# Laying out the setup of a two-layer transformer kernel by VectorE's time, and cutting its norms into pieces

## The chip, the cores and the metric

The kernel runs on one core of a Trainium2 chip. The metric is the device time of one execution in microseconds; of several runs the median is taken. Everything is computed in 32-bit floats.

## The reference

Two transformer layers follow one another on x of shape (8, 512, 256), with a condition of shape (8, 256) and a context of shape (8, 64, 192). The kernel's text calls them block 0 and block 1. Cut to what matters:

```
# layer 0 (16 heads of 16)
mod = silu(cond) @ adaln_w.T + adaln_b          # split in nine: shift, scale, gate of sa, ca, ff
h = ln(x) * (1 + scale_sa) + shift_sa
q, k, v = ln(heads(h)), ln(heads(h)), heads(h)  # no projection, a norm of every head
x = x + gate_sa * unheads(softmax(q k^T / 4) v)
h = ln(x) * (1 + scale_ca) + shift_ca
kv = ctx @ cond_w.T + cond_b
x = x + gate_ca * (softmax((h wq^T)(kv wk^T)^T / 4)(kv wv^T) @ ca_out_w.T + ca_out_b)
h = ln(x) * (1 + scale_ff) + shift_ff
x = x + gate_ff * ((silu(h @ w1.T) * (h @ w3.T)) @ w2.T)
# layer 1 (16 heads of 64, rotary positions on q and k)
a = ln(x) * (1 + cond @ g1 + ..) + (cond @ b1 + ..)
x = x + attention(a, a) ;  x = x + attention(adaln1(x), ln(ctx)) ;  x = x + gelu(adaln2(x) w1) w2
```

## The kernel before

Each of the 8 batch elements ("batches") of x is kept in SBUF as four tiles of 128 tokens by 256 features. Block 0 is worked as a list of slots, which `run_blocks` walks through. In slot i it issues the early functions of the slot's block, the scores of block i (TensorE), the values of block i−1, and then whatever `beside` holds for slot i, a dictionary to which `at(i, fn)` appends. Within this loop the order on TensorE, VectorE, ScalarE and GpSimd is exactly the order in which the code issues instructions (`manual_schedule`); SyncE's queue, which issues the DMAs, is ordered by a scheduler. An instruction that waits therefore holds up everything behind it on its own engine.

A cycle has 18 slots. Batch b's self-attention in block 0 takes 16 slots from `base = 18 b` on: four head groups, each with four blocks of 128 keys. The other two slots of a cycle hold the two cross-attention blocks of the batch before. So in the steady state three batches are in work at once:

- `batch1(b)`: self-attention. `norm` normalizes and modulates x into `h`; `head_centre`, `head_var` and `head_scale` do the norm of every head (a power on GpSimd, 16 or 32 elements per partition); `queries_keys` transposes (L500) and evicts q on ScalarE (L503) and k on VectorE (L504). Exponentials are L520; `group_back` divides by the sums (L547 to L549).
- `batch2(b)`: cross-attention, from `base = 18 (b+1)`. `prepare` at base+3 normalizes x to z (statistics L183/L184, rstd L174 on VectorE, its power L175 on GpSimd, four applications L187) and adds a row to x (L395). `turn` at base+5 transposes z (L362) and evicts it with scale and shift (L363). `queries` at base+6 and base+7 are two projections with w_q (L609 evicts them). `inverse` takes the reciprocal of the sums and sends it through DRAM and back over all partitions (DMAs `rec`, `rb`); `scaled` multiplies (L652), and the output projection (w_o, in bank `ps_D`) opens the next cycle but one.
- `batch3(b)`: the feed-forward part, from `base = 18 (b+2)`, a few slots later for some batches and two earlier for the last: `prepare` at base+5, `turn` at base+7, eight `up` steps, then four `down` steps, whose results are added with a gate (L418, L420).

Ahead of slot 0 and within the first 18 slots lies the setup. `linear_rows` multiplies the conditions' 8 rows with 512 columns of the modulation's weights and adds the biases on VectorE (L258). The first modulation row is spread over the 128 partitions by a matmul with ones. `to_columns` transposes rows into columns (L263). `awake` issues matmuls whose results nobody reads. `modulation` (slot 1) makes the other rows, `context0` (3), `keys0` (5) and `values0` (7 to 10) the cross-attention's keys and values, `modulation1` (12) and `context1` (14) the conditions and the context of block 1. This setup up to slot 0 is ordered by the scheduler.

In the second cycle `keys1(p)`, at slots 20, 22, .. 34, makes the cross-attention keys of block 1: two matmuls, rotary positions on VectorE and GpSimd (L735 to L739), and a store to DRAM (`k_d`, L759). At slot 36 `open_ff` loads the feed-forward weights.

All matmuls go through one helper, so they share L109 in the profile. Accumulators are the banks `ps_S`, `ps_O`, `ps_D` and `ps_X`.

Of the kernel before, what the change touches and what calls it, by code (L numbers as in the profile page):

```python
# [10 lines left out]
F32 = mybir.dt.float32  # L11
# [67 lines left out]
def fast_path(ctx: ExitStack, tc: tile.TileContext, a: dict, out: bass.AP):  # L79
# [109 lines left out]


# [20 lines left out]
    nc.sync.dma_start(cT, a["cT"].rearrange("(k p) b -> p k b", p=P))  # L211
    mod = sp.tile([B, 9 * D], F32, name="mod")
    nc.sync.dma_start(mod, a["adaln_b"].to_broadcast([B, 9 * D]))
    adaw = sp.tile([P, 2, 9 * D], F32, name="adaw")

# [3 lines left out]
    load_k(adaw[:, :, 0 : 2 * D], a["adaln_wT"][:, 0 : 2 * D])  # L219
    load_x(0)  # L220
    nc.sync.dma_start(cols, a["cols"])
    load_k(adaw[:, :, 2 * D : 3 * D], a["adaln_wT"][:, 2 * D : 3 * D])
    load_k(adaw[:, :, 3 * D :], a["adaln_wT"][:, 3 * D :])

    ctxT = sp.tile([96, 2, B * T], F32, name="ctxT")
    condw = sp.tile([96, 2, D], F32, name="condw")
    wk0 = sp.tile([P, 2, D], F32, name="wk0")
    wv0 = sp.tile([P, 2, D], F32, name="wv0")
    gb = sp.tile([B, 4 * D], F32, name="gb")
    gbw = sp.tile([P, 2, 4 * D], F32, name="gbw")  # L230
    ctx_in = sp.tile([P, 4, CD], F32, name="ctx_in")

    def load_rest():
        load_k(ctxT, a["ctxT"], 96)
        load_k(condw, a["cond_wT"], 96)
        nc.sync.dma_start(ctx_in, a["ctx"].rearrange("(t p) d -> p t d", p=P))
        load_k(wk0, a["wkT"])
        load_k(wv0, a["wvT"])
        nc.sync.dma_start(rows, a["rows"].to_broadcast([P, 5 * D]))
        nc.sync.dma_start(gb, a["gb_b"].to_broadcast([B, 4 * D]))  # L240
        load_k(gbw, a["gb_w"])
        load_k(w_q0, a["wqT"])
        load_k(w_o0, a["woT"])
        for b in range(1, B):
            load_x(b)


    scT = sp.tile([P, 2, B], F32, name="scT")
    nc.scalar.activation(scT, cT, AF.Tanh, scale=0.5)
    nc.vector.scalar_tensor_tensor(scT, scT, 1.0, cT, ALU.add, ALU.mult)  # L250
    nc.vector.tensor_scalar_mul(scT, scT, 0.5)

    def linear_rows(dst, xT, w, lo, n):

        ps = bank_x()
        for kc in range(2):
            mm(ps[:B, :n], xT[:, kc, :], w[:, kc, lo : lo + n], kc == 0, kc == 1)
        nc.vector.tensor_tensor(dst[:, lo : lo + n], ps[:B, :n], dst[:, lo : lo + n], ALU.add)  # L258

    def to_columns(dst, src, chunks):  # L260
        ps = bank_x()
        for i, lo in enumerate(chunks):
            nc.tensor.transpose(ps[:, i * B : (i + 1) * B], src[:, lo : lo + P], ident[:B, :B])  # L263
        nc.vector.tensor_copy(dst.rearrange("p c b -> p (c b)"), ps[:, : len(chunks) * B])

    def awake(n):

        ps = bank_s()
        for _ in range(n):
            mm(ps[:, 0, 0:256], ident, chk.rearrange("p i c -> p (i c)"))  # L270

    awake(4)
    linear_rows(mod, scT, adaw, 0, 512)
    nc.vector.tensor_scalar_add(mod[:, SC_SA : SC_SA + D], mod[:, SC_SA : SC_SA + D], 1.0)
    first_mod = bank_x()
    mm(first_mod, ones, mod[0:1, 0 : 2 * D])
    linear_rows(mod, scT, adaw, 512, 256)
    nc.sync.dma_start(modd[:, 0 : 3 * D], mod[:, 0 : 3 * D])
    awake(13)
    for h in hs:  # L280
        nc.gpsimd.memset(h, 0.0)
        nc.gpsimd.memset(h[:, :, :, HD0 : HD0 + 1], 1.0)
    nc.vector.tensor_copy(qk_cols, cols[:, 0:2])

    def modulation():
        for lo in range(3 * D, 9 * D, 512):
            linear_rows(mod, scT, adaw, lo, 512)

        nc.vector.tensor_scalar_mul(mod[:, G_FF : G_FF + D], mod[:, G_FF : G_FF + D], 0.5)
        nc.sync.dma_start(modd[:, 3 * D :], mod[:, 3 * D :])  # L290
        to_columns(modT, mod, [lo + k * P for lo in (SH_CA, SC_CA, SH_FF, SC_FF) for k in range(2)])
        for lo in (2, 6):
            nc.vector.tensor_scalar_add(modT[:, lo : lo + 2, :], modT[:, lo : lo + 2, :], 1.0)
# [4 lines left out]
    def context0():  # L298
        nc.gpsimd.memset(vb0, 0.0)
        for m in range(2):  # L300
            ps = bank_x()
            for kc in range(2):
                mm(ps, condw[:, kc, m * P : (m + 1) * P], ctxT[:, kc, :], kc == 0, kc == 1)
            nc.vector.tensor_scalar_add(kvT[:, m, :], ps, col("condb")[:, m : m + 1])

    def keys0():
        for m in range(2):
            ps = bank_x()
            for kc in range(2):
                mm(ps, wk0[:, kc, m * P : (m + 1) * P], kvT[:, kc, :], kc == 0, kc == 1)  # L310
            for e in range(2):
                nc.vector.tensor_scalar(kb0[:, m, :, e, :], ps.rearrange("p (b t) -> p b t", b=B),
                                        col("bk")[:, m : m + 1], col("parity")[:, e : e + 1], ALU.add, ALU.mult)
# [12 lines left out]

    def modulation1():

        for lo in range(0, 4 * D, 512):
            linear_rows(gb, cT, gbw, lo, 512)  # L330
        gbT = sp.tile([P, 8, B], F32, name="gbT")
        to_columns(gbT, gb, [k * P for k in range(8)])
# [11 lines left out]
    def context1():  # L344
        for k in range(2):
            ps = bank_x()
            for t in range(4):
                nc.tensor.transpose(ps[:96, t * P : (t + 1) * P], ctx_z[:, t, k * 96 : (k + 1) * 96], ident)
            nc.vector.tensor_scalar(ctxzT[:, k, :], ps[:96, :], col("lncw")[:96, k : k + 1],
                                    col("lncb")[:96, k : k + 1], ALU.mult, ALU.add)  # L350
# [15 lines left out]
    def normed_in_pieces(pool, b, eps):  # L366

        z = pool.tile([P, NT, D], F32, tag="z", name="z", bufs=1)
        st = small.tile([P, NT, 6], F32, tag="st", name="st")
        mv = small.tile([P, NT, 2], F32, tag="mv", name="mv")  # L370
        x, r = xs[b], {}

        def stats(t0):
            for t in range(t0, t0 + 2):
                nc.vector.bn_stats(st[:, t, :], x[:, t, :])
            for t in range(t0, t0 + 2):
                nc.vector.bn_aggr(mv[:, t, :], st[:, t, :])
            if t0:
                r[0] = rstd_of(mv[:, :, 1], NT, eps)

        def apply():
            for t in range(NT):
                nc.vector.tensor_scalar(z[:, t, :], x[:, t, :], mv[:, t, 0:1], r[0][:, t : t + 1],
                                        ALU.subtract, ALU.mult)

        return z, [lambda: stats(0), lambda: stats(2), apply]
# [53 lines left out]
    def batch1(b):  # L440
# [3 lines left out]
        def norm(half=None):  # L444

            if not half:
                s["bc"] = bc = wk.tile([P, 3 * D], F32, tag="bc", name="bc")
                spread(bc, b, SH_SA, 3 * D)
                s["h"] = hs[b % 2]
                s["hv"] = s["h"][:, :, :, 0:HD0]  # L450
                s["ln"] = ln = wk.tile([P, NT, D], F32, tag="ln", name="ln", bufs=1)
                layernorm(ln, xs[b], EPS0)
            lo, n = (0, D) if half is None else (half * P, P)
            eng, rows_ = (nc.gpsimd, s["bc"]) if b else (nc.vector, first_mod)
            ln = s["ln"][:, :, lo : lo + n]
            eng.tensor_tensor(ln, ln, rows_[:, None, D + lo : D + lo + n].to_broadcast([P, NT, n]), ALU.mult)
            lv = ln.rearrange("p t (h d) -> p t h d", d=HD0)
            shift = rows_[:, lo : lo + n].rearrange("p (h d) -> p h d", d=HD0)
            eng.tensor_tensor(s["hv"][:, :, lo // HD0 : (lo + n) // HD0], lv,
                              shift[:, None].to_broadcast([P, NT, n // HD0, HD0]), ALU.add)  # L460

        def head_centre(c):

            if c == 0:
                s["z"] = wk.tile([P, NT, DX], F32, tag="zx", name="zx", bufs=1)
                nc.gpsimd.memset(s["z"][:, :, D:DX], 0.0)
            hv = s["hv"][:, :, 8 * c : 8 * c + 8]
            z = s["z"][:, :, c * P : (c + 1) * P]
            zv = z.rearrange("p t (h d) -> p t h d", d=HD0)
            sh = [P, NT, 8]  # L470
            mean = small.tile(sh, F32, tag="mean", name="mean", bufs=2)
            nc.vector.tensor_reduce(mean, hv, AX.X, ALU.add)
            nc.vector.tensor_scalar_mul(mean, mean, 1.0 / HD0)
            nc.vector.tensor_tensor(zv, hv, mean[:, :, :, None].to_broadcast([*sh, HD0]), ALU.subtract)
# [1661 lines left out]
```

## Time and profile before

| | |
|---|---|
| median of 3 runs | 2459.03 us (2456.31 to 2459.05) |
| profiled execution, own time | 2458.86 us |
| its span | 2457.1 us |
| TensorE busy | 2409.4 us (98%) |
| VectorE / ScalarE / GpSimd busy | 1070.0 / 875.8 / 859.1 us |
| mean granted clock of TensorE | 0.995 |
| DMA | 84.33 MB, 34 GB/s on average |
| first scores of slot 0 / 18 / 36 start at | 25.52 / 101.06 / 170.88 us |

The span runs from the first to the last recorded instruction. Busy times count the records of an engine; a record of TensorE that runs at half the clock counts as busy for twice as long. The profile shows block 0 in about the first third of the span; the rest is block 1.

### The profile page before, as it was taken

How to read it: one execution, taken by the hardware profiler on the slowest of the kernel's cores; microseconds unless marked ns; L12 is line 12 of the kernel's file. 1: busy time of each engine (PE TensorE's matmuls, PEld its weight loads, DVE VectorE, ACT ScalarE, POOL GpSimd, SP SyncE). 2: the span in 40 equal slices, each digit the busy share in tenths (PEclk: the TensorE clock that was granted, in tenths of full speed). 3: DMA queues.
4: the chain of work that ended last, by engine and by line, in shares of the span. 5: the costliest groups of instructions: out<-in, count | busy, mean ns of one | idle time of the engine just before them, and what ended most of it. 6: DMA issues, size and time to landing. Idle time of an engine off the chain costs nothing.

```text
span 2457.1 us, 28357 instructions
## 1 busy us (share of the span) xinstructions
PE 2409.4 (98%) x10938; PEld 1151.5 (47%) x10938; DVE 1070.0 (44%) x2074; ACT 875.8 (36%) x1115; POOL 859.1 (35%) x537
## 2 busy tenths in 40 slices
PE   8999999999999999999999999999999999999999
PEld 3323444434435543444444443434345555566665
DVE  4555444444434534343434343434335666651210
ACT  2555545555462124333333333333332221222221
POOL 3542332332201026343434344444433443531110
PEclk9999999999999999999999999999999999999999
DMA  5121000000001100000000000000113222210000
GB/s 184 32 76 34 17 11 12 21 7 16 13 6 39 56 1 23 19 18 19 19 19 19 19 19 19 19 19 19 36 56 101 68 67 62 68 53 29 22 18 23
DMA packets 84448, 84.33 MB, mean 34 GB/s; under 512 B 42416, under 2 KB 58736, under 8 KB 84296
## 3 DMA queue, kind: packets, MB, share of 16 engines
q1 hardware_dynamic: 83688, 81.88, 10.7%
q8 instruction: 88, 1.44, 0.2%
q10 hardware_dynamic: 616, 0.55, 0.1%
q14 instruction: 56, 0.46, 0.1%
HBM read 72.36 MB, written 10.04 MB: 34 GB/s over the span
## 4 chain that ended last, share of the span: by engine, by line
PE 91%; DVE 2%; DMA 2%; ACT 2%; issue 1%; POOL 1%; SPq 1%; POOLq 0%; DVEq 0%; ACTq 0%
PE ps_X L109 37%; PE ps_S L109 23%; PE ps_D L109 14%; PE ps_O L109 14%; DMA rb<-rec 1%; PE ps_X L362 1%; ACT p L520 1%; POOL p L1148 1%; SPq L1141 1%; DMA rec<-rec 1%; DVE t L738 1%; PE ps_X L500 0%; ACT hT L363 0%; PE ps_X L542 0%; POOL rstd L491 0%
## 5 line engine op out<-in xcount | busy, mean ns | idle before, releaser
L109 PE MATMUL ps_S<-q,k 32*128 32x512 f32 (+1 forms) x3072 | 432.2, 627 | 7.0 <-ACT p L520 3.4
L908 ACT ACTIVATE p<-ps_S 128x1024 f32<-128x1024 f32 x256 | 248.2, 1022 | 522.2 <-PE ps_S L109 520.3
L520 ACT ACTIVATE p<-ps_S 128x1024 f32<-128x1024 f32 x256 | 248.2, 1021 | 259.9 <-PE ps_S L109 259.0
L109 PEld LDWEIGHTS ps_S<-q,k 32*128 32x128 f32 (+1 forms) x3072 | 160.2, 185 | 244.6 <-issue 134.4
L887 DVE TENSOR_TENSOR t<-ps_X,rope_c 128x512 f32<-128x512 f32 x126 | 87.2, 692 | 349.9 <-PE ps_X L109 349.9
L927 DVE TENSOR_TENSOR sm<-sm,p 128x1024 f32<-128x1024 f32 x128 | 191.8, 1541 | 58.5 <-ACT p L908 58.5
L890 POOL TENSOR_TENSOR q<-t 128x512 f32<-128x512 f32 x32 | 40.7, 1273 | 406.2 <-DVE t L888 406.2
L175 POOL TENSOR_TENSOR rstd<-rstd,mhalf 128x4 f32<-128x4 f32 x49 | 49.8, 1016 | 364.8 <-DVE rstd L174 363.4
L923 POOL TENSOR_TENSOR sm<-p 128x1024 f32<-128x1024 f32 x64 | 149.5, 2362 | 37.8 <-ACT p L908 37.8
L109 PE MATMUL ps_X<-hT,w 128*128 128x512 f32 x344 | 160.3, 601 | 0.9 <-ACT hT L363 0.4
L739 POOL TENSOR_TENSOR q<-t,t 128x512 f32<-128x512 f32 x72 | 94.9, 1319 | 174.3 <-DVE t L738 163.1
L109 PE MATMUL ps_O<-p,h 128*32 128x512 f32 x1024 | 139.0, 615 | 0.5 <-ACT oT L533 0.5
L109 PE MATMUL ps_O<-p,v 128*64 128x512 f32 x512 | 138.0, 617 | 0.0
L109 PE MATMUL ps_D<-p,v 128*64 128x512 f32 x512 | 131.6, 592 | 0.0
L411 DVE TENSOR_TENSOR x<-ps_X,x 128x512 f32<-128x512 f32 x27 | 18.7, 691 | 241.3 <-PE ps_X L109 241.3
L109 PE MATMUL ps_X<-hT,w_sa_wq 128*128 128x512 f32 x256 | 115.9, 595 | 3.0 <-ACT hT L363 3.0
L109 PE MATMUL ps_X<-w_sa_wv,hT 128*128 128x512 f32 x256 | 118.0, 604 | 0.0
L109 PE MATMUL ps_X<-w_sa_wo,oT 128*128 128x256 f32 x512 | 114.5, 382 | 0.1
L109 PE MATMUL ps_X<-hT,w_sa_wk 128*128 128x512 f32 x248 | 112.4, 596 | 0.0
L109 PE MATMUL ps_S<-hT,w_ff_w 128*128 128x512 f32 x256 | 111.3, 593 | 0.0
L491 POOL TENSOR_TENSOR rstd<-var,mhalf 128x32 f32<-128x32 f32 (+1 forms) x17 | 87.3, 5134 | 68.6 <-ACT t L692 41.7
L109 PEld LDWEIGHTS ps_X<-w_sa_wo,oT 128*128 128x128 f32 x512 | 96.0, 190 | 24.2 <-issue 11.4
(256 smaller groups left out, 3536.5 us busy)
## 6 DMA issues: line engine op xcount, KB each, us to landing
rb<-rec SPq DMA_DIRECT2D x128, 128.0 KB
rb<-rec_d SPq DMA_DIRECT2D x124, 128.0 KB
x<-in_x_dram SPq DMA_DIRECT2D x8, 512.0 KB
rb<-rec SPq DMA_DIRECT2D x16, 256.0 KB
out_dram<-x SPq DMA_DIRECT2D x15, 256.0 KB
bc<-modd SPq DMA_DIRECT2D x8, 384.0 KB
gate<-modd SPq DMA_DIRECT2D x16, 128.0 KB
k_d<-q SPq DMA_DIRECT2D x8, 256.0 KB
```

What stands on the lines that cost most here:

```text
L109: nc.tensor.matmul(o, lhsT, rhs, start=start, stop=stop)
L175: nc.gpsimd.tensor_tensor(r[:, :n], r[:, :n], mhalf[:, :n], ALU.pow)
L362: nc.tensor.transpose(ps[:, t * P : (t + 1) * P], z[:, t, k * P : (k + 1) * P], ident)
L491: nc.gpsimd.tensor_tensor(r, s["var", c][:, :, hd], half, ALU.pow)
L520: nc.scalar.activation(pr[u], pss[u], AF.Exp, scale=HD0 ** -0.5)
L738: nc.vector.tensor_tensor(t2[d], ps[src], sn[src].to_broadcast([64, *shape[1:]]), ALU.mult)
L739: nc.gpsimd.tensor_tensor(dst, t1, t2, ALU.add)
L887: nc.vector.tensor_tensor(c, ps, rope_c, ALU.mult)
L890: nc.gpsimd.tensor_tensor(r[0], ec, os, ALU.subtract)
L908: nc.scalar.activation(pr, pss[u], AF.Exp, scale=HD1 ** -0.5)
L923: nc.gpsimd.tensor_tensor(sm, s["p", g, 0, u], s["p", g, 1, u], ALU.add)
L927: nc.vector.tensor_tensor(s["sm", g, u], s["sm", g, u], s["p", g, t, u], ALU.add)
```

## The change

The change edits the issue order and the cutting of block 0's work; block 1's own phases issue what they issued.

- **Setup in program order.** The manual order now begins ahead of the setup. The first modulation weights come in two DMAs from ScalarE's queue, batch 0's x in four. The modulation is held as a tile of four groups of 32 rows: eight products of 32 columns with 32 zero-padded conditions, in place of six with 8 rows. Batch 0's modulation row is made on TensorE alone, from its condition repeated over 128 columns, plus ones times bias, plus ones. `awake` runs with 6, 16, 3 and 3 matmuls, in bank O. Fills with zeros are cut to the parts that need them.
- **First heads of batch 0.** The first 8 heads are cut by parity: the even ones go ahead of slot 0 (256 elements per partition, their scaling on VectorE), the odd ones lie in slots 0 and 1, the other 8 heads in slots 2 to 4.
- **The other setup steps** lie in other slots: `modulation` 1, its columns 3, its end 4, `context0` 4 and 5, `keys0` 7 and 9 (half of its eviction on ScalarE), `values0` 10, 11, 14, 15, the context's norm 10, 11, 13, `modulation1` 15, its columns 16, `context1` 16 and 17, the rest of `modulation1` at slot 54.
- **Norms of block 0 in three pieces** (statistics of two tiles; of the other two, and rstd; application): for `batch1` at three successive slots, for `batch2` at base+3, +4, +5, with `turn` at base+6 and the queries at base+7 and +8; for `batch3` at base+4, +5, +7 (the last batch: all at base+5).
- **`keys1(p)`** at slots 22 to 29, one a slot, their stores four slots later, with five buffers.

```diff
+    def norm_pieces(dst, x, eps, width=D):
+        s = {}
+        def stats(t0):
...
+            for t in range(t0, t0 + 2):
+                nc.vector.bn_stats(s["st"][:, t, :], x[:, t, :])
+            for t in range(t0, t0 + 2):
+                nc.vector.bn_aggr(s["mv"][:, t, :], s["st"][:, t, :])
+            if t0:
+                s["r"] = rstd_of(s["mv"][:, :, 1], NT, eps)
+        def apply():
+            d = dst()
...
+        return [lambda: stats(0), lambda: stats(2), apply]
...
+    ms.enter_context(tc.manual_schedule(engines={ENG.PE, ENG.DVE, ENG.Activation, ENG.Pool}))
+    nc.sync.dma_start(cT, a["cT"].rearrange("(k p) b -> p k b", p=P))
+    for k in range(2):
+        nc.scalar.dma_start(adaw[:, k, 0 : 2 * D], a["adaln_wT"][k * P : (k + 1) * P, 0 : 2 * D])
+    for t in range(NT):
+        nc.sync.dma_start(xs[0][:, t, :], a["x"][0][t * P : (t + 1) * P, :])
...
+    awake(6)
+    for k in range(2):
+        mm(first_mod, sc0[:, k, :], adaw[:, k, 0 : 2 * D], k == 0, False)
+    mm(first_mod, ones, mod[0:1, 0 : 2 * D], False, False)
+    mm(first_mod[:, D : 2 * D], ones, chk[0:1].rearrange("p i c -> p (i c)"), False, True)
+    awake(16)
-    awake(4)
-    linear_rows(mod, scT, adaw, 0, 512)
-    nc.vector.tensor_scalar_add(mod[:, SC_SA : SC_SA + D], mod[:, SC_SA : SC_SA + D], 1.0)
-    first_mod = bank_x()
-    mm(first_mod, ones, mod[0:1, 0 : 2 * D])
-    linear_rows(mod, scT, adaw, 512, 256)
-    nc.sync.dma_start(modd[:, 0 : 3 * D], mod[:, 0 : 3 * D])
-    awake(13)
...
     def modulation():
-        for lo in range(3 * D, 9 * D, 512):
-            linear_rows(mod, scT, adaw, lo, 512)
+        ps = bank_x()
+        for k in range(2):
+            for j in range(4):
+                mm(ps[32 * j : 32 * j + 32, :], sc32[:, k, :], adaw[:, k, 2 * D * j : 2 * D * j + 2 * D], k == 0, k == 1)
+        nc.vector.tensor_tensor(mod[:, 0 : 2 * D], ps, mod[:, 0 : 2 * D], ALU.add)
...
-                        at(-1, lambda: head_scale(0, 0))
-                        at(0, lambda: head_scale(0, 1))
-                        at(0, lambda: norm(1))
+                            first_modulated(0, 0)
+                            head_centre(0, 0)
+                            head_var(0, 0)
+                            head_scale(0, 0, nc.vector)
...
+                        at(0, lambda: first_modulated(0, 1))
+                        at(0, lambda: head_centre(0, 1))
+                        at(1, lambda: head_var(0, 1))
+                        at(1, lambda: head_scale(0, 1))
...
-                        at(i - 10, norm)
+                        for m in range(3):
+                            at(i - 11 + m, lambda m=m: norm(m))
...
-        at(base + 3, prepare)
-        at(base + 5, turn)
-        at(base + 6, lambda: queries(0))
-        at(base + 7, lambda: queries(1))
+        for n in range(3):
+            at(base + 3 + n, lambda n=n: prepare(n))
+        at(base + 6, turn)
+        at(base + 7, lambda: queries(0))
+        at(base + 8, lambda: queries(1))
...
-        at(base + 5, prepare)
-        at(base + 7, turn)
+        for n, i in enumerate((5, 5, 5) if b == B - 1 else (4, 5, 7)):
+            at(base + i, lambda n=n: prepare(n))
+        later.append((base + 7, turn))
...
-        at(CYCLE + 2 + 2 * p, lambda p=p: keys1(p))
+        at(CYCLE + 4 + p, lambda p=p: keys1(p))
+        at(CYCLE + 8 + p, lambda p=p: store_keys1(p))
```

## The prediction

> **What bounds the kernel now.** I read the page's busy times first:
>
> ```profile
> PE 2409.4 (98%) x10938; PEld 1151.5 (47%) x10938; DVE 1070.0 (44%) x2074; ACT 875.8 (36%) x1115; POOL 859.1 (35%) x537
> ```
>
> The span is 2457.1 us, so TensorE is idle for 47.7 us in all. The table of windows says where these are, and where busy time is slow time (PEclk is the column after POOL):
>
> ```profile
> 20.00:30.00 10.00, 4.11 (x19) 1.81 (x20) 3.65 (x6) 2.71 (x3) 6.49 (x4) 0.72 1.04 358
> 30.00:40.00 10.00, 9.81 (x32) 2.00 (x28) 2.85 (x5) 2.46 (x3) 5.61 (x2) 0.76 0.79 252
> 80.00:100.00 20.00, 17.74 (x92) 6.48 (x94) 11.43 (x34) 8.93 (x13) 9.49 (x4) 0.83 0.24 64
> 150.00:200.00 50.00, 45.76 (x256) 16.52 (x258) 26.73 (x67) 28.60 (x35) 26.39 (x13) 0.93 0.31 107
> 200.00:250.00 50.00, 49.88 (x238) 17.93 (x231) 24.20 (x62) 28.03 (x37) 13.65 (x8) 1.00 0.03 7
> ```
>
> From 200 us on TensorE has 49.88 of 50 us: nothing to win there, but any wait put there goes straight to the end. Before 200 us there are idle gaps, and three spells at half clock: smaller windows show 0.50 from about 24.5 to 35.3, 86.0 to 93.2 and 181.7 to 188.2 us. The waits of TensorE name what opens the gaps:
>
> ```profile
> PE ps_D L109 <- DVE oT L652: 3.3, 1, 3.3
> PE ps_X L500 <- POOL zx L492: 3.1, 1, 3.1
> PE ps_S L109 <- DVE k L504: 2.3, 2, 1.7
> PE ps_D L263 <- DVE gb L258: 2.1, 2, 1.9
> ```
>
> **The change, part by part.** All sums stand against the profiled execution, 2458.86 us (span 2457.1 and 1.76 around it; the median of the runs, 2459.03, is 0.17 away). Names below are those of the kernel before.
>
> *The start.* The chain to the first scores, in the timeline:
>
> ```profile
> 14.74 0.69 DVE L456 TENSOR_TENSOR ln<-ln,ps_X 128x512 f32<-128x512 f32 x1 [1.21 <-PE ps_X L109]
> ...
> 19.49 2.90 POOL L491 TENSOR_TENSOR rstd<-var,mhalf 128x16 f32<-128x16 f32 x1 [8.58 <-DVE var L482]
> 22.48 0.62 POOL L492 TENSOR_TENSOR zx<-zx,rstd 128x256 f32<-128x256 f32 x1
> 23.15 0.66 PE L500 MATMUL ps_X<-ident,zx 128*128 128x128 f32 x4 [3.07 <-POOL zx L492]
> ...
> 25.52 1.24 PE L109 MATMUL ps_S<-q,k 16*128 16x512 f32 x4 [1.71 <-DVE k L504]
> ```
>
> x lands at 7.26; its DMA was issued at 2.13, behind the bias load (0.40 us of issue) and the weights (0.40). Now the weights go from ACT's queue and x in quarters: some 0.9 earlier, 6.4. Statistics and rstd (2.26 from landing to the rstd's start in the row of before, with the pieces overlapping their loads less), POOL's power 1.03 and four applies 1.38 then end at 9.9 instead of 12.2. The modulation row no longer passes through DVE: two matmuls (1.02 each at full clock), ones times bias (1.12) and half of that again, behind six waking matmuls that end at 6.8 (8 cold records took 3.53, so 12 take 5.3 from about 1.5): 10.5. From there the chain is halved in width: modulate and centre on 256 elements (0.42 for what took 0.69) 2.0 instead of 3.1, square 0.40, variance 0.6, power 2.90 unchanged, scale on DVE 0.42, transposes 0.66, q and k 0.78 + 0.81. First scores 19.9 instead of 25.52: **−5.6**. Bounds: 18.9 (the row ready with the applies at 9.9, and q beside k) to 21.5 (the two matmuls at half clock, 1.86 each as in the row at 5.88).
>
> *Slots 0 to 17.* Before, they take 75.54 us (25.52 to 101.06), of which TensorE is busy 70.40 and idle 5.14. The two half-clock spells (10.8 and 7.3 us) stretched their work by half their length, 9.05; so the work is 61.35 at full clock. The modulation's six 8-row products (6.4 us of records, biases' columns included) become eight side-by-side 32-column products, 3.5 by the time of four ordinary ones; the second block's four (4.6) become 1.5; two `awake(3)` add 6 × 0.454 = 2.7 (24 records took 5.45): 58.05. Idle: the 1.90 at `gb` goes (its addition and columns lie in different slots now); of the other 3.24 I keep three quarters, 2.4. New waits: the parity-1 heads' POOL power (2.90) begins only after slot 0's DVE work, transposes wait 1.15; centre operations of batch 1 ahead of the setup's DVE work in slots 13 and 14, 1.0; its squares ahead of an exponential in slot 15, 2.0. Together 64.6, slot 18 at 84.5 instead of 101.06: with the start **−16.5**. Bounds: −18.5 (old idle gone altogether), −13.5 (waits doubled). The spells vanish because their causes do: the 3.07 gap before L500 is filled by `awake(16)`, the 1.90 gap by spreading.
>
> *Keys of the second block, a slot each, stores four slots later.* Same eight products. Cycle 1 takes 72.79 with 71.67 busy; I take −1.0 (0 to −2.7: RoPE's POOL and DVE operations, 1.32 and 0.69 each, come twice as densely). Their stores leave SP's queue before the first reciprocal's round trip (two DMAs, `rec` and `rb`) needs it. Before, the first output projection waited for it:
>
> ```profile
> 176.65 0.60 PE L109 MATMUL ps_D<-w_o,oT 128*128 128x256 f32 x2
> 180.53 2.03 PE L109 MATMUL ps_D<-w_o,oT 128*128 128x256 f32 x6 [3.29 <-DVE oT L652]
> ```
>
> The 3.29 go, and with them the half-clock spell of 6.5 behind them (3.25 lost); less about 1.0 because the weights of the feed-forward part are still queued there: **−5.5** (−3.3 if the spell stays, −6.6 if the wait goes whole).
>
> *Norms in pieces, in the full cycles.* The third piece (`apply`) of the cross-attention's norm moves to two slots after the first, its transposes from slot base+5 to base+6, the queries one slot on. In cycle 3 now:
>
> ```profile
> 391.41 0.60 PE L362 MATMUL ps_X<-ident,z 128*128 128x128 f32 x4
> ...
> 392.11 0.42 DVE L549 TENSOR_TENSOR attn<-ps_X,inv 128x256 f32<-128x256 f32 x1
> ...
> 394.44 0.66 PE L500 MATMUL ps_X<-ident,zx 128*128 128x128 f32 x4
> ```
>
> z is ready a slot early today (its last apply ends at 390.2). After, z's apply is queued on DVE behind the head group's division (0.17 + 0.25 + 0.42 + two checks, 0.99, starting at 391.61), the feed-forward norm's second statistics (1.05) and rstd (0.17 + about 0.2), and takes 1.38 to 1.79: 395.4 as the middle. With the old transposes out of slot 77, TensorE reaches z's transposes at about 394.0, behind L500's. It stands 1.45 there (1.1 to 2.2), and everything after it on its queue stands too: scores, so exponentials, so values. Batches 1 to 5 (slots 42, 60, 78, 96, 114) have this: **+7.5** (5.5 to 11). Batch 0 is in cycle 1, without a feed-forward norm beside it; batches 6 and 7 meet fewer operations.
>
> *The tail of block 0.* Around batch 7's cross norm TensorE has only down products left:
>
> ```profile
> 758.70 7.07 PE L109 MATMUL ps_D<-w,hid 128*128 128x256 f32 x32
> ...
> 763.79 1.79 DVE L187 TENSOR_SCALAR z<-x,mv,rstd 128x256 f32<-128x256 f32 x4 [1.13 <-POOL rstd L175]
> 765.60 1.04 PE L362 MATMUL ps_X<-ident,z 128*128 128x128 f32 x8
> 765.80 0.69 DVE L418 TENSOR_TENSOR tmp<-ps_D,gate 128x512 f32<-128x512 f32 x1 [0.22 <-PE ps_D L109]
> ```
>
> The whole norm (760.2 to 765.6) hides under the 7.07 now. Cut in pieces over three slots, its second piece comes on DVE after L418/L420, which wait for the last down product (765.77). So after that: 0.69 + 0.72 + statistics 1.05 + rstd 0.2 + POOL 1.1 + apply 1.4 to 1.8 = 5.4 on average, with 0.2 of starts 5.6, all of it TensorE's. A spell at half clock follows by the rows above (6.5 us: 3.25; 5.3 at least: 2.2), 2.8 in the middle: **+8.4** (5.7 to 9).
>
> Sum: −16.5 − 1.0 − 5.5 + 7.5 + 8.4 = −7.1: 2451.8 us. All best ends give −16.6 (2442.3), all worst +3.2 (2462.1).
>
> **A rule beside a row.** Whether the new waits trip the clock decides more than their length. In the rows, 3.29 and 3.07 idle were followed by 0.50, but so was 1.90 beside eight tiny 8x8 transposes. The Trainium skill, "TensorE: Matmul & The Clock Gate", section "HAM oscillation — how this bites in real kernels", allows idle gaps up to about 3.4 us before the clock is halved; by it all three gaps would have been safe, so the trace is stricter. By the page the five waits cost their length alone and the tail's 5.6 would be the only spell; by the strictest row, each of the five brings a spell.
>
> **The rivals.** (B) *The cycle waits hide.* ScalarE's pair of exponentials takes 1.94 to 2.04, and the DVE order may be loose enough that apply ends with L500. The 7.5 go: 2444.3. For it: DVE is idle more than half of these cycles. Against: strict order on each engine puts three fixed pieces ahead. (C) *The start's gain is halved.* One of the new waits in slots 0 to 17, or the idle at the very start, brings back a half-clock spell, and the parity chain waits on POOL: 8.25 less, 2460.0. For it: 0.50 appeared twice in this stage with waits of this size. (D, slower) *The 1.45 waits trip the clock.* One mechanism, slots 42 to 114: each wait is followed by a spell like 181.7 to 188.2, 6.5 to 7.3 us, 3.4 lost: 5 × 3.4 = +17, 2468.8. It decides as soon as three of five trip (+10 against −7.1). For it: the 1.90 row. Against: behind that gap stood eight transposes that keep the array little busy, while these have dense matmuls on both sides.
>
> **How the numbers follow.** A measurement of this kernel can tell about 0.2%, 4.9 us, so faster is under 2454.0 and slower over 2463.8. The forecast (own range 2446 to 2458) gets 0.52, B 0.17, C 0.14, D 0.17. Some seven tenths of the forecast's mass and B are faster: 0.53. The rest of the forecast and most of C: 0.28. D and the edge of C: 0.19. The range 2442 to 2464 leaves out D and a little of B.
>
> **What would show it.** Right: first scores near 19.9, slot 18 near 84.5, PEclk 1.00 from 20 to 100 us and from 180 to 190; a wait of about 1.45 of z's transposes for DVE's apply, five times; about 5.6 idle near 750 with 0.50 behind it. Wrong: 0.50 after the five waits (D), no such waits (B), 0.50 inside the first 80 us (C); or a wait for a DMA in the first cycles, which nothing here has priced.

## The result, and the profile after

The changed kernel takes 2449.36 us (median of 6 runs, 2447.73 to 2451.98) against 2457.67 (2453.98 to 2461.03) for the kernel before in the same comparison: ratio 0.9967, 95% interval 0.9955 to 0.998. That is 8.3 us; forecast were 7.1. The profiled execution has a span of 2446.9 instead of 2457.1. But several terms of the sum were wrong and cancelled, which is luck, as a ledger of marks shows. A mark is the start of the first exponential of a head group in block 0; the last two rows lie in block 1.

| mark | before, us | after, us | difference |
|---|---|---|---|
| batch 0, first head group | 27.64 | 20.41 | −7.23 |
| batch 1, first head group (slot 18) | 102.29 | 86.38 | −15.91 |
| batch 2, first head group (slot 36) | 172.11 | 159.40 | −12.71 |
| batch 2, fourth head group | 244.91 | 228.85 | −16.06 |
| batch 3, 4, 5, 6, first head group | 269.77, 366.62, 463.48, 560.33 | 253.71, 351.38, 449.05, 546.71 | −16.06, −15.25, −14.43, −13.62 |
| batch 7, first head group | 657.18 | 644.37 | −12.82 |
| block 1, an exponential of its self-attention | 906.17 | 898.33 | −7.84 |
| block 1, last exponential | 2202.59 | 2192.47 | −10.11 |

The page's line for TensorE (busy us, share of the span, instructions):

```profile
PE 2408.0 (98%) x10964; PEld 1157.3 (47%) x10964; DVE 1058.9 (43%) x2083; ACT 878.5 (36%) x1118; POOL 858.5 (35%) x538
```

TensorE's busy time is down by only 1.4 us; its idle time fell from 47.7 to 38.9. The windows show where (TensorE's busy time first; the number after POOL is the granted clock):

```profile
20.00:30.00 10.00, 8.69 (x62) 3.19 (x58) 3.95 (x10) 6.12 (x7) 3.52 (x2) 1.00 1.04 361
...
60.00:80.00 20.00, 17.48 (x106) 6.35 (x104) 13.37 (x44) 10.16 (x12) 11.61 (x6) 0.91 0.00 1
80.00:100.00 20.00, 20.00 (x133) 6.99 (x130) 5.24 (x14) 15.86 (x18) 9.54 (x4) 1.00 0.31 83
...
150.00:200.00 50.00, 47.11 (x262) 17.73 (x257) 21.46 (x61) 29.72 (x35) 19.96 (x11) 0.90 0.16 48
200.00:250.00 50.00, 49.88 (x235) 19.51 (x234) 20.62 (x47) 25.04 (x33) 17.83 (x7) 1.00 0.04 13
```

The spells of 24.5 and 85.9 are gone. In their place there is a short one of 3.4 us at 74.8, and 150 to 200 is worse than before in clock (0.90 against 0.93): a spell of 10.2 us from 156.7 on. The waits of TensorE, one line for each cause:

```profile
PE ps_D L416 <- DVE z L208: 4.5, 1, 4.5
...
PE ps_S L109 <- ACT p L574: 3.1, 7, 2.1
PE ps_S L109 <- DVE k L558: 3.0, 3, 2.1
...
PE ps_X L554 <- POOL zx L546: 1.3, 1, 1.3
```

The old waits on `zx` (3.1), `gb` and `oT` are off the list or small. New are z at the end of block 0 (4.5), one wait of 2.1 on exponentials (slot 15), and one of 2.1 on k (slot 35). The start's chain, in the timeline:

```profile
10.02 0.42 DVE L516 TENSOR_TENSOR ln<-ln,ps_X 128x256 f32<-128x256 f32 x1 [0.37 <-PE ps_X L109]
...
13.27 2.90 POOL L545 TENSOR_TENSOR var<-var,mhalf 128x16 f32<-128x16 f32 x1 [5.11 <-DVE var L539]
16.21 0.42 DVE L546 TENSOR_TENSOR zx<-zx,var 128x256 f32<-128x256 f32 x1 [3.02 <-POOL var L545]
16.92 0.60 PE L554 MATMUL ps_X<-ident,zx 128*128 128x128 f32 x4
...
19.24 1.14 PE L109 MATMUL ps_S<-q,k 16*128 16x512 f32 x8 [0.42 <-DVE k L558]
```

First scores at 19.24, forecast 19.9: the modulation row was ready at 10.02 instead of 10.5, and the steps behind it have about the lengths that they were given. In the full cycles, this is the place of the wait that the forecast put at 1.45 us (cycle of batch 4):

```profile
376.86 0.42 DVE L603 TENSOR_TENSOR attn<-ps_D,inv 128x256 f32<-128x256 f32 x1
...
378.43 1.38 DVE L208 TENSOR_SCALAR z<-x,mv,rstd 128x256 f32<-128x256 f32 x4
...
378.64 0.66 PE L554 MATMUL ps_X<-ident,zx 128*128 128x128 f32 x4
...
379.13 1.05 PE L416 MATMUL ps_X<-ident,z 128*128 128x128 f32 x4
```

VectorE begins the application at 378.43, 0.2 us before TensorE begins its transposes of zx, and the four transposes of z need one tile each: they run behind the four applications at their pace, 1.05 us instead of 0.60. That is 0.45 of waiting that no wait row of the matmuls shows (the rows of the weight loads, PEld, show 0.18 of it twice). The same place at the end of block 0:

```profile
745.46 7.07 PE L109 MATMUL ps_X<-w,hid 128*128 128x256 f32 x32
...
752.56 0.69 DVE L460 TENSOR_TENSOR tmp<-ps_X,gate 128x512 f32<-128x512 f32 x1 [4.61 <-PE ps_X L109]
...
755.14 1.02 POOL L175 TENSOR_TENSOR rstd<-rstd,mhalf 128x4 f32<-128x4 f32 x1 [13.30 <-DVE rstd L174]
...
756.20 1.78 DVE L208 TENSOR_SCALAR z<-x,mv,rstd 128x256 f32<-128x256 f32 x4 [1.13 <-POOL rstd L175]
757.06 1.44 PE L416 MATMUL ps_D<-ident,z 128*128 128x128 f32 x4 [4.53 <-DVE z L208]
```

VectorE is idle for 4.61 us until the last down product lets the addition go, and the norm's second half and its application come behind it, as forecast. TensorE starts again at 757.06, 0.9 us before the last of the four applications ends (757.98). And this is the stretch around slot 35, which no step of the forecast had (queue of SyncE, VectorE, TensorE):

```profile
142.93 0.40 SPq L253 DMA_DIRECT2D w<-in_w1T_dram  x1
143.39 0.57 SPq L253 DMA_DIRECT2D w<-in_w3T_dram  x1
...
144.61 0.34 SPq L724 DMA_DIRECT2D rec<-rec  x1
...
144.99 0.56 SPq L253 DMA_DIRECT2D w<-in_w2T_dram  x1
...
150.75 0.67 SPq L726 DMA_DIRECT2D rb<-rec  x1
...
155.67 0.69 DVE L729 TENSOR_TENSOR oT<-oT,rb 128x512 f32<-128x512 f32 x1 [8.19 <-DMA rb<-rec]
...
156.28 0.81 DVE L558 TENSOR_SCALAR k<-ps_D,cols 128x512 f32<-128x512 f32 x1
...
157.23 2.09 PE L109 MATMUL ps_S<-q,k 16*128 16x512 f32 x8 [2.09 <-DVE k L558]
```

The three feed-forward weight loads of 1 MB each are issued around the reciprocal's store. The reciprocal's broadcast `rb` is issued 6.1 us after that store and has landed 4.9 us later. VectorE stands 8.19 us in front of it, with k queued behind.

### The profile page after: what moved, and what is told of

Read it like the earlier page. It is cut to its first block, busy times and chain, and to the rows that moved or that the text cites. A ratio compares the mean times of both kernels' runs of the same rounds, so it can differ in the third digit from the quotient of the medians.

```text
span 2446.9 us, 28449 instructions
## 1 busy us (share of the span) xinstructions
PE 2408.0 (98%) x10964; PEld 1157.3 (47%) x10964; DVE 1058.9 (43%) x2083; ACT 878.5 (36%) x1118; POOL 858.5 (35%) x538
## 4 chain that ended last, share of the span: by engine, by line
PE 92%; DVE 3%; issue 1%; ACT 1%; DMA 1%; POOL 1%; SPq 0%; POOLq 0%; DVEq 0%; ACTq 0%
PE ps_X L109 38%; PE ps_S L109 23%; PE ps_O L109 14%; PE ps_D L109 14%; PE ps_X L416 1%; DVE t L836 1%; DMA rec<-rec 1%; DMA rb<-rec 1%; POOL p L1252 1%; ACT p L574 0%; PE ps_X L554 0%; PE ps_X L596 0%; PE ps_D L416 0%; DVE t L833 0%; ACT hT L417 0%
## 5 line engine op out<-in xcount | busy, mean ns | idle before, releaser
L453 DVE TENSOR_TENSOR x<-ps_X,x 128x512 f32<-128x512 f32 x27 | 18.7, 692 | 239.4 <-PE ps_X L109 239.4
L545 POOL TENSOR_TENSOR var<-var,mhalf 128x32 f32<-128x32 f32 (+1 forms) x17 | 87.3, 5135 | 75.2 <-ACT t L773 41.7
```

What stands on the lines that cost most here:

```text
L545: nc.gpsimd.tensor_tensor(var, var, half, ALU.pow)
```

## The experiments

Each was measured beside the kernel before; ratios are to that. Where marks are given they come from the one profiled execution.

**The weights out of the way.** The changed kernel with

```diff
-            load_k(w, a[name])
+    def load_ff():
...
+            nc.scalar.dma_start(w, a[name].rearrange("(k p) f -> p k f", p=P))
...
+    at(2 * CYCLE + 3, load_ff)
```

> The changed kernel with one edit: the three 1 MB feed-forward weight loads are issued from ScalarE's queue in slot 39, instead of from SyncE's queue around slot 31. Theory (collision): in the changed kernel those loads stand ahead of the first reciprocal's broadcast (rb issued 150.75, landed 155.67), so VectorE's scaling holds k back, TensorE waits 2.09 us at 157.23, and a spell of half clock (156.7 to 166.9) follows. Without the collision the 2.09 wait and the spell of 10.2 us (5.1 lost) are gone: the start of batch 2's third head group 5 to 7 us earlier than in the changed kernel (191.3 there), the end near 2442. Rival (density): the second block's keys, one a slot, fill VectorE and GpSimd, and that makes k late; then the wait at k stays at about 2 and the time stays at 2449.

2447.13 us, ratio 0.9948 (0.9932 to 0.9965). The stretch of slot 35, VectorE's scaling and the same scores:

```profile
152.35 0.69 DVE L729 TENSOR_TENSOR oT<-oT,rb 128x512 f32<-128x512 f32 x1 [3.32 <-DMA rb<-rec]
...
156.91 2.04 PE L109 MATMUL ps_S<-q,k 16*128 16x512 f32 x8 [0.17 <-DVE chk L146]
```

and its clock (1.00) in the 6 us from 160 on:

```profile
160.00:166.00 6.00, 6.00 (x40) 2.89 (x44) 3.05 (x8) 2.80 (x5) 2.60 (x2) 1.00 0.10 39
```

In the changed kernel the same line reads

```profile
160.00:166.00 6.00, 6.00 (x28) 1.72 (x21) 0.69 (x1) 3.78 (x5) 0.00 (x0) 0.50 0.13 46
```

Wait and spell are gone. Batch 2's third head group starts at 187.44 instead of 191.31, although this execution was already 1.56 late at slot 18, where its spell at 73.4 lasted 6.8 us instead of 3.4: 5.4 us for the edit. Density is refuted. The edit changes the queue of the loads and their time together; which of the two does it was not tried. The end was expected near 2442 and came 5 later, in part because the two spells that are left, at 73.4 and in the tail, lasted 6.8 each here, for 3.4; the effect is read between the marks.

**The keys back.**

```diff
-        at(CYCLE + 4 + p, lambda p=p: keys1(p))
-        at(CYCLE + 8 + p, lambda p=p: store_keys1(p))
+        at(CYCLE + 2 + 2 * p, lambda p=p: keys1(p))
+        at(CYCLE + 2 + 2 * p, lambda p=p: store_keys1(p))
```

> The changed kernel with the second block's keys back where they were, slots 20, 22, .. 34, each stored in its own slot. Both theories, collision and density, expect no wait at k in slot 35, because the feed-forward weights can then only load after the last keys. They differ behind it: collision expects the old wait back (the first output projection for the scaled oT, about 3.3, with a spell at half clock of 6.8), so that slots 18 to 38 gain nothing against the changed kernel: 2449, within 2. Density expects the whole 7 us of the k wait and its spell to be saved: 2442.

2449.49 us, ratio 0.9962 (0.9948 to 0.9977). The wait for the scaled oT is back, 2.74 us at 163.83, without a spell behind it; batch 2's third head group starts 2.6 us earlier than in the changed kernel (3.05, of which 0.45 were there from the start). In this pair of executions the early keys, as the change made them, cost some 2.6 us; but there was a spell of 10.2 us in one and none in the other, the medians differ by 0.1 only (2449.49 and 2449.36), and with the old norms ("The old norms" against "The setup alone", below) the same stretch, from slot 18 to batch 2's third head group, is 1.0 shorter with early keys (103.22 us against 104.25). So with the weights where the change left them, the early keys are worth nothing that these runs can tell. Here the weights are issued at 160.35, behind both broadcasts: where the keys go, the weights go, since they take over the keys' memory.

**The keys back, with the weights out of the way and the old norms** (the two edits above, and the next one):

> The faster variant (norms at their old places, weights loaded from ScalarE's queue in slot 39) with the second block's keys back at slots 20, 22, .. 34. If early keys have a worth of their own once the weights are out of the way (their stores no longer between the reciprocals), the first output projection waits for the scaled oT here by about 2 to 3 us and the start of batch 2's second head group is 2 to 6 us later than in that variant (169.34): 2436 to 2440. If the collision was the whole matter and the keys' place is worth nothing, it is the same within 1 us there: 2434.

2441.72 us, ratio 0.9937 (0.9921 to 0.9953). Batch 2's second head group starts at 174.63, 5.3 us later than in the variant with early keys. SyncE's queue shows where it starts: VectorE had the reciprocal ready at 154.98, but its store is issued at 157.22, behind a store of the keys (with early keys, ready at 153.50 and issued at 153.53), and another store of the keys stands ahead of the broadcast:

```profile
156.81 0.32 SPq L859 DMA_DIRECT2D k_d<-q  x1
157.22 0.38 SPq L724 DMA_DIRECT2D rec<-rec  x1
158.03 0.32 SPq L859 DMA_DIRECT2D k_d<-q  x1
159.06 0.63 SPq L726 DMA_DIRECT2D rb<-rec  x1
```

The first output projection then waits 2.73 us (at 163.74), and 3.4 us at half clock follow. The early keys are worth 5.3 us at this mark once the weights don't take it back (0.8 of it up to slot 36); the forecast had 6.5, 1.0 of it for cycle 1. The medians differ by 7.9.

**The old norms.**

```diff
-            at(base + 3 + n, lambda n=n: prepare(n))
-        at(base + 6, turn)
+            at(base + 3, lambda n=n: prepare(n))
+        at(base + 5, turn)
...
-        for n, i in enumerate((5, 5, 5) if b == B - 1 else (4, 5, 7)):
-            at(base + i, lambda n=n: prepare(n))
-        later.append((base + 7, turn))
+        for n in range(3):
+            at(base + 5, lambda n=n: prepare(n))
+        at(base + 7, turn)
```

The two `queries` lie one slot earlier, as `turn` does.

> The changed kernel with the cross-attention's and the feed-forward part's norms back at their old places (all three pieces at base+3 and at base+5, transposes at base+5 and base+7, queries at base+6 and base+7). Theory: the pieces cost 0.81 us in each of the cycles of batches 2 to 6 and about 5 us around the last cross norm (4.53 wait and a spell of 3.4 at half clock). Both go: block 0 ends 8.2 us earlier than in the changed kernel, 2441. Rival: the 0.81 comes from the new order of the transposes alone and the tail only moves its wait to the next product; then under 4 us: 2446 or more.

2440.43 us, ratio 0.9921 (0.9905 to 0.9938): 8.9 less than the changed kernel's median. The marks gain 0.81 in every cycle (−2.91 at batch 3, −3.72, −4.53, −5.34, −6.15 at batch 7), and the last exponential of block 0 ends 11.7 us earlier than in the changed kernel. Of these, 9.6 are left at the mark in block 1 (888.71): a new spell of 3.4 us begins at 803.0. The old norms gain in cycle 1 too, where the sum charged the pieces nothing: from slot 18 to batch 1's fourth head group it takes 57.02 us instead of 58.51, and the same 57.02 instead of 58.50 between the run with both repairs and the one with the weights out of the way.

**The last batch's norm alone in one slot.**

```diff
-            at(base + 3 + n, lambda n=n: prepare(n))
+            at(base + 3 + (n if b < B - 1 else 0), lambda n=n: prepare(n))
```

> The changed kernel with all three pieces of the last batch's cross norm in one slot (base+3), nothing else. If the order of the second piece behind the last down product's addition is the cause of the 4.53 us wait at 757.06, the wait is under 0.5 and the spell at half clock behind it is gone: 5 us less at the first block's end, 2444. If VectorE is late there for another reason (the old place is itself behind that addition), a wait of over 3 stays.

2446.43 us (one run). The down products and what follows them:

```profile
745.95 7.07 PE L109 MATMUL ps_X<-w,hid 128*128 128x256 f32 x32
752.85 0.60 PE L416 MATMUL ps_D<-ident,z 128*128 128x128 f32 x4
```

The 4.53 us are gone, and the spell behind them; the last exponential of block 0 ends at 774.78 instead of 780.54, having started the cycle 0.49 later: 6.2 us for the tail. At the mark in block 1, 4.2 of them are left (894.67): here too a new spell of 3.4 us follows, at 809.5.

**The setup alone**: the old norms and the old place of the keys together.

> The changed kernel with the second block's keys and all norms of cross-attention and feed-forward back at their old places: of the change only the setup, the first heads and the pieces of the self-attention's norm are left. If these carry the gain (16 us up to slot 18 in the changed kernel) and the other two parts only took away from it, block 0 ends about 19 us earlier than in the kernel before and the time is 2438 to 2441. If the other two parts contributed to the gain, it is slower than 2446.

2439.68 us, ratio 0.9929 (0.9912 to 0.9945). The setup carries more than the whole gain, 18.7 us. As they were made, the norms gave some 9.8 of it back (2449.49 with the new norms and the old place of the keys), and the early keys changed nothing that can be told (2440.43 with the old norms).

**Both repairs**: the old norms and the weights from ScalarE's queue, keys early.

> The changed kernel with the norms back at their old places and the feed-forward weights loaded from ScalarE's queue in slot 39; the keys stay early. If the two edits add up (8.9 us and 5.4 us in their stages when made alone), 2435. If the collision's wait returns with the old norms in another form, 2440 as with the norms alone.

2433.86 us, ratio 0.9899 (0.9883 to 0.9916): what was expected if the two edits add up.

**Filler in the old kernel.**

```diff
-    awake(13)
+    awake(20)
```

> The kernel before with one number changed: the second group of waking matmuls has 20 instead of 13, 3.2 us more, so TensorE works through the idle 20.08 to 23.15. If that idle time opened the first spell at half clock (24.5 to 34.7, 10.2 us), the spell goes and slot 1 to 18 start 5 us earlier: 2454. If the spell comes from the thin work after it (1.71 and 1.11 us of waits around the first scores), it stays and the time is 2459.

2454.07 us (10 runs), ratio 0.9983 (0.9974 to 0.9993): the time that was expected if the spell goes. But the profiled execution (2456.62, the slowest of the ten) shows another way there:

```profile
30.00:34.00 4.00, 4.00 (x15) 0.56 (x12) 0.69 (x2) 2.57 (x3) 0.00 (x0) 0.50 1.11 351
...
180.00:190.00 10.00, 8.41 (x52) 4.13 (x54) 7.05 (x16) 4.09 (x5) 5.05 (x2) 1.00 1.02 369
```

The first spell is still there, later and shorter (29.4 to 36.2, 6.8 us). The spell at 181 is missing, with the wait for oT in front of it still 3.39 us. So this run doesn't settle what opened the first spell.

**No filler at the new start**: the changed kernel without its line `awake(16)`.

> The changed kernel without its sixteen waking matmuls ahead of the first transposes, so TensorE is idle for about 7 us, 9.9 to 16.9. If the filler is what keeps the clock up, a spell of 3.4 to 10 us at half clock covers the first slots and slot 4 starts 2 to 5 us later than in the changed kernel (34.09 there). If the three matmuls before slot 0 and the three in slot 0 are enough, slot 4 starts within 1 us of it.

2454.30 us (one run). The clock (after the five busy times) in the first slots:

```profile
10.00:14.00 4.00, 0.00 (x0) 0.00 (x0) 2.12 (x7) 0.42 (x1) 1.08 (x1) 0.70 1.02 343
14.00:20.00 6.00, 3.67 (x14) 2.66 (x14) 2.06 (x5) 0.78 (x1) 1.82 (x1) 0.50 1.10 335
20.00:26.00 6.00, 6.00 (x23) 2.79 (x22) 1.03 (x4) 1.94 (x2) 0.00 (x0) 0.56 1.02 367
```

A spell of 13.7 us from 11.6 on; slot 4 starts at 37.28 instead of 34.09, slot 18 at 91.03 instead of 86.38 (its spell at 76.4 lasted 6.8 too). In this one run the filler is what keeps the clock, and its worth is 3.2 us at slot 4.

**Filler in slot 14.** To the variant with both repairs, `at(14, lambda: awake(4))`.

> The faster variant (norms at their old places, weights loaded from ScalarE's queue in slot 39) with four more waking matmuls, 1.82 us, at the end of slot 14, inside the 2.05 us for which TensorE waits at 72.58 for exponentials. If idle time of that length is what drops the clock, the spell at half clock (3.4 at 74.9) goes and slot 18 starts 1.7 us earlier than the 86.38 there (the wait itself stays): 2432. If the filler delays the matmuls behind it as much as it saves, 86.4 and 2434.

2436.03 us, ratio 0.9911 (0.9897 to 0.9925): slower by 2.2 than without the filler, as neither expected.

```profile
74.92 2.47 PE L109 MATMUL ps_O<-chk,ident 128*128 128x256 f32 x5 [4.39 <-DVE chk L146]
```

The filler multiplies the tile `chk`, into which VectorE's checks of the sums write. It waited for one of them, and slot 18 started 3.4 us late. The next run multiplies the identity with itself, seven times:

> The faster variant again with filler at the end of slot 14, now seven matmuls of the identity with itself (about 1.8 us), which read nothing that VectorE writes; the four of the run before read the tile that VectorE's checks write, and waited 4.39 us for one. If idle time of 2.05 us is what drops the clock here, the spell at 74.9 goes and slot 18 starts 1.7 us earlier than 86.38: 2432. If the spell comes from more than that one gap, it stays and slot 18 starts at 86.4 or later: 2434.

2432.18 us, ratio 0.99 (0.9884 to 0.9917), the lowest median of all, though its interval can't be told from that of the variant without filler. The filler, the scores behind it, and two windows:

```profile
70.65 1.72 PE L109 MATMUL ps_O<-ident 128*128 128x128 f32 x14
72.86 2.04 PE L109 MATMUL ps_S<-q,k 16*128 16x512 f32 x8 [0.49 <-ACT p L580]
```

```profile
72.00:75.40 3.40, 2.91 (x20) 0.93 (x18) 3.28 (x15) 3.03 (x4) 3.27 (x1) 1.00 0.00 0
75.40:78.80 3.40, 3.40 (x20) 1.57 (x16) 1.24 (x5) 0.64 (x1) 3.32 (x3) 0.50 0.00 0
```

TensorE now idles for 0.49 instead of 2.05, and the spell comes all the same. Slot 18 starts at 86.66, having started at 20.75 instead of 20.46: nothing gained there. It is not shown that the lower median comes from the filler; this profile also lacks the spell at 798.5 that the variant without filler has. So the length of that gap alone is not what drops the clock in slot 15; the last section has an estimate of what may.

**The changed kernel once more.**

> The changed kernel once more, to tell what its profiled execution gained in the second block's cross-attention (2.2 us between 1830 and 2130 us, a stage that the change doesn't touch). If it is chance of one execution, this one ends that stage within 0.5 us of the kernel before, counted from 900 us on, and the medians differ by 8 as before. If the change moved it, the 2.2 us are there again.

2451.68 us, ratio 0.9971 (0.996 to 0.9982): 6.9 less than the kernel before, for 8.3 the first time. From 900 us to the last exponential it gains 2.2 us on the kernel before, as the first profile did (−6.53 to −8.72; −7.84 to −10.11), so it isn't chance of that one execution. In the filler run of the old kernel, which has the old block 1, that stretch is 0.5 shorter than in the profile of before, so the reference is a little slow itself. What moved the other 1.7 us is open: it was not tried.

## Why the prediction was right, and where it was wrong

The sign, the size and the range held: 8.3 us for 7.1 forecast. That the total came so near is luck: in the profiled executions the steps were off by up to 4.9 us, in both directions.

- *Start and slots 0 to 17*: −16.5 forecast, −15.9 at the mark. Scores came 6.3 us earlier for 5.6 forecast. The slots gave 9.6 for 10.9: the wait at 29.61 was 1.31 (forecast 1.15), the one of slot 15 2.05 (2.0), but behind this one stood a short spell that the sum didn't have, and at 53.51 an unpriced 1.57 for ScalarE's copy.
- *Cycle 1 and the first projection*, up to batch 2's fourth head group: −5.0 forecast (−6.5 for the keys, and +1.5 for the first of the five cycle waits, at slot 42, which lies in this stretch), −0.15 measured (−15.91 to −16.06). This is the step that failed, and the term in it is "less about 1.0 because the weights of the feed-forward part are still queued there". With the keys' memory given back earlier the weights load earlier (142.93, where before it was 176.82), ahead of the first broadcast; the wait moved from the projection to k, and its spell lasted 10.2 us, for 6.8 before. Priced as the runs show it, the early keys are worth 5.3 and the collision costs 5.4. The cross-attention's norm in pieces also cost 1.5 in cycle 1, which the sum put at nothing for batch 0.
- *The five cycle waits*: +7.5 forecast (five times 1.45 is 7.25), 0.81 a cycle measured, +3.2 over the last four, for which 6.0 were forecast. 0.45 of each is the wait at z; most of the rest lies at the scores of the slot before, which take 1.46 us (376.26) instead of 1.14 (392.38 before), now that no transposes of z stand ahead of them. The mechanism is right and its size was off. VectorE came earlier: the whole application ended 0.7 us after TensorE got there (379.81 against 379.13), not 1.45. And the sum made TensorE wait for the whole application (1.38 to 1.79), while the trace shows it released tile by tile. At 0.45 us each the waits gave rival D, the spells behind waits of 1.45, nothing to act on.
- *The tail*: +8.4 forecast, 5.0 by the marks of before and after (6.2 by the run that takes it away). The wait was 4.53 for 5.6, for the same reason of tiles, and its spell 3.4 us long (1.7 lost, for 2.8).

By the marks, 0.6 and 4.9 us too much credit, in the first and the second of these steps, stood against 2.8 and 3.4 too much charge on the norms: −7.84 in block 1 for −7.1. Behind that mark, where the sum had nothing, the profile gained another 2.3. One reading was off too: the forecast took the two old spells up to slot 18 as 10.8 and 7.3 us, but the clock's changes stand at 24.47, 34.71, 85.91 and 92.74, so they were 10.24 and 6.83 long and took 8.5 us, not 9.05. Rival B, hidden cycle waits, was half true; C's place for a spell (the first 80 us) was real, at a fifth of its price.

The clock rule of the Trainium skill ("TensorE: Matmul & The Clock Gate", "HAM oscillation — how this bites in real kernels") fared so: of the waits under its 3.4 us, those of 1.31, 1.57 and 1.17 in the changed kernel left the clock alone, as it says. Against it, the waits of 1.9 to 2.1 on exponentials and on k were followed by 0.50 in every profile that has them, and where filler cut the first of them to 0.49 the spell stayed. At one place near 800 us every profile has a wait of 1.1 to 1.9 ahead of transposes of z: in four (1.53 to 1.61) a spell followed, in six with 1.58 to 1.91 none did. A wait of 3.39 for oT was followed by none. Neither the page's bound nor the strictest row of the prediction decides by the length of one gap.

## What to carry to other kernels

Price a moved step by what its memory releases as well as by what it issues: a buffer given back earlier lets the next loads go earlier, and here 3 MB of them shared the queues with a 256 KB broadcast on which an in-order engine hung. When a consumer works tile by tile, charge it with the first tile of its producer and the difference in pace, not with the whole producer. And when a change has several parts, run each alone: here one part carried the gain, and repairing the other two gave 15 us more.

## What the runs showed that was not expected

- Spells at half clock last a multiple of 3.4 us: 3.4, 6.8, 10.2 and 13.7 were seen. In each of the 14 profiles all changes of the granted clock lie on one grid with steps of 3.413 us: in the changed kernel the spells begin at 74.75, 156.67 and 757.42, which are 24 and 176 steps apart. From one execution to the next the grid lies elsewhere. One and the same wait was followed by 3.4 in one execution and 6.8 in another (slot 15), or by 6.8 and by none (the wait for oT at 180 in the old kernel, 3.29 and 3.39). A single profile is uncertain by about 1.7 us for each such place.
- How much of the array a step of that grid uses sorts the spells better than any gap. This is an estimate from the trace's records: for each step, add up the columns that the matmuls stream, each times its share of the 128 rows and 128 columns of the array (the scores, `16*128`, count an eighth). A dense step holds about 4100. The steps just ahead of all 34 spells hold 1466 or less (649, 1446 and 138 in the changed kernel). Of the 9880 steps at full clock that no spell follows, eight hold so little: seven in the two profiles of the old kernel, all with products of 8 columns in them, and one of 1463. It fits the pairs above: the wait of 3.29 for oT left 886 in one step, while the one of 3.39 was split over two, the lower with 1574; near 800 us the four steps ahead of a spell hold 1375 to 1466, the others 1671 or more. No run was made to test it.
- Keeping TensorE issuing is not enough: with seven small identity products (fourteen records) in the gap, the clock of slot 15 dropped as before. By the estimate the step from 72.02 on, busy for 86% of its time, held only 1382: most of the filler (70.65 to 72.37) lay in the step before.
- Filler matmuls have operands too: four that read a tile written by VectorE cost 3.4 us.
